# Keys before queries in the first batch, 1/rms spread through DRAM, and one add for the last shared expert tokens

## The chip, the cores and the metric

The kernel runs on one core of a Trainium2 chip. The metric is the device time of one execution in microseconds (us). A core has five engines that work through lists of their own: TensorE (PE; its weight loads are shown as PEld), VectorE (DVE), ScalarE (ACT), GpSimd (POOL) and SyncE (SP). DMAs are issued from the lists of SP, ACT and POOL ("SPq", "ACTq", "POOLq" in the profile) and move data beside them.

## The reference

Everything is float32. `x` is [4, 512, 512], the context [4, 1601, 512]; the first 257 context rows are image, the other 1344 text.

```python
def rms_norm(x, w):   # over all 512 features, before the heads are split
    return x * rsqrt(mean(x * x, -1) + 1e-6) * w

# 1. cross attention, 16 heads of 32
xl = layernorm(x)
q = rms_norm(xl @ q_w.T + q_b, norm_q_w)
k, v = rms_norm(ctx_txt @ k_w.T + k_b, norm_k_w), ctx_txt @ v_w.T + v_b
k_img, v_img = rms_norm(ctx_img @ k_img_w.T + k_img_b, norm_k_img_w), ctx_img @ v_img_w.T + v_img_b
x = x + (attention(q, k, v) + attention(q, k_img, v_img)) @ o_w.T + o_b    # two softmaxes

# 2. mixture of experts on layernorm(x): T = 2048 tokens, 32 experts
#    4 experts a token, chosen in the best 3 of 8 groups; at most 80 tokens an expert, in token order
out[token] += weight * down(silu(gate(x)) * up(x))       # routed experts, inner size 256
out += shared_down(silu(shared_gate(x)) * shared_up(x))  # shared expert, inner size 512
return x + out
```

## The kernel before, in words

The kernel writes its order out by hand: Python code appends instructions to the engines' lists, and nothing reorders them. PSUM is a ring of eight banks (`psum()`); a bank is used again when its readers are done. A float32 matmul of 512 columns stands in the trace as two records.

**Opening.** `first_x` loads four x tiles, then `wq` (four pieces), `first_wk`, `first_block` and the other weights, all from SP's queue; ScalarE's queue loads biases and norm weights (`column`, `bias_column`), 512 single floats each for a bias. `queries(0, ...)` gives for each x tile the steps `measure` (VectorE and GpSimd), `norm` (ScalarE, `xl`) and `turned` (transposes on TensorE, copied to `xlT` by ScalarE), and `work`, the four chunks of the query projection. All of it precedes the batch loop for batch 0; for later batches it is done in the batch before.

**Keys of one batch.** The keys are made transposed, features on partitions, in `BLOCKS` of 512, 512, 320 and 257 keys and four chunks of 128 features. `keys(bl, c)` makes one chunk: matmuls over four k (`feature_chunk`), then ScalarE squares the result (`sq`), VectorE adds the bias and multiplies by the norm weight (L228), GpSimd adds up the squares (L230). `norms` (in `side`: `N(x)`) sums the squares over partitions with a matmul against ones (L239), VectorE copies the sums out (L241) and GpSimd makes 1/rms of them (`inv_sqrt`, L196 and L197), as [128, 4]: one number for each key or query. `normed` (`M(x)`) has TensorE spread these numbers over all partitions (L250: a broadcast lhsT against the identity), and VectorE multiplies all four chunks with the result in PSUM (L253). `W(bl, qt)` are the scores of head group 0 for one block and one query tile: four matmuls in four banks (L299), whose largest values VectorE takes (L302). The table `side` says which of these steps follows which chunk; `select` are VectorE's routing steps of two batches before, seven behind a chunk. Then a list of steps follows: the rest of the scores, value tiles (`val`, copied from PSUM by ScalarE), for batches after the first the residual work of the batch before (`R(qt, i)`), `split` (VectorE) and `shifts`, which begins with transposes (L351).

**Attention.** For each of four chunks `c` of heads and 13 key tiles: exponentials on ScalarE (L366), weighted sums on TensorE (L373), denominators added up by GpSimd or VectorE (L381), the next chunk's scores (`wave`, L314 and L328).

**Experts.** `shared()` gives the steps of the shared expert for each 512 tokens: `gate`, `up`, `down`. The first three batches' steps are done before the routed experts. The 12 steps of the last (`between`: four gates, four ups, four downs) are spread through the loop over the routed experts. Such a `down` is copied from PSUM by ScalarE (`ys`) and added to `out` in DRAM by one of GpSimd's DMAs (L946). For a routed expert `gather(e)` fetches the rows of its tokens (L965, GpSimd's queue), `turn` transposes them (L976), `gate_up` and `down` are matmuls (L217, L995), ScalarE scales the result to `y` (L999), and an indirect DMA of GpSimd's queue adds it to `out` (L1000). Each DMA that adds to `out` waits until the one before has landed. `AHEAD` is how many experts ahead the rows are fetched, `WEIGHTS` how many experts' weights (1.5 MB each, from SP's queue) have a place.

Of the kernel before, what the change touches and what calls it, by code (L numbers as in the profile page):

```python
# [9 lines left out]
F32 = mybir.dt.float32  # L10
# [48 lines left out]
@with_exitstack  # L59
def xattn_moe_kernel(ctx: ExitStack, tc: tile.TileContext, a: dict, out: bass.AP):  # L60
    nc = tc.nc

    dram = ctx.enter_context(tc.tile_pool(name="dram", bufs=1, space=DRAM))
    x1_d = dram.tile([T, D], F32, name="x1_d")

    xw_d = dram.tile([T, D + E], F32, name="xw_d")
    xnT_d = dram.tile([P, NC, T], F32, name="xnT_d")
    den_d = dram.tile([B * NC, 2 * NG4, L], F32, name="den_d")
    rec_d = dram.tile([B * NC, 2 * NG4, L], F32, name="rec_d")

    const = ctx.enter_context(tc.tile_pool(name="const", bufs=1))
    ident = const.tile([P, P], F32, name="ident")
    make_identity(nc, ident)
    mhalf = const.tile([P, 8], F32, name="mhalf")
    nc.gpsimd.memset(mhalf, -0.5)
    logits = const.tile([P, NT, E], F32, name="logits")

    with tc.manual_schedule():
        body(tc, a, ident, mhalf, logits, x1_d, xw_d, xnT_d, den_d, rec_d, out)
# [30 lines left out]
def body(ctx, tc, a, ident, mhalf, logits, x1_d, xw_d, xnT_d, den_d, rec_d, out):  # L110
# [55 lines left out]
    def load_x(b, qt):  # L166
        xt = rowt("xt")
        nc.sync.dma_start(xt, a["x"][b, qt * P:(qt + 1) * P, :])
        return xt
# [64 lines left out]
    def norms(sq, n):  # L234

        nsub = -(-n // P)
        ps = psum()
        for s in range(nsub):
            nc.tensor.matmul(ps[:, s:s + 1], lhsT=sq[:, s * P:(s + 1) * P], rhs=ones[:, 0:1], start=True, stop=True)  # L239
        r = st.tile([P, 4], F32, name="rrms")  # L240
        nc.vector.tensor_copy(r[:, :nsub], ps[:, :nsub])  # L241
        inv_sqrt(r[:, :nsub], r[:, :nsub], 1.0 / D, 1e-6)
        return r

    def normed(dst, r, n):

        ps = psum()
        for s in range(-(-n // P)):
            m = min(P, n - s * P)
            nc.tensor.matmul(  # L250
                ps[:, s * P:s * P + m], lhsT=r[:, s:s + 1].to_broadcast([P, P]), rhs=ident[:, :m], start=True, stop=True
            )
        nc.vector.tensor_tensor(dst, dst, ps[:, :n].unsqueeze(1).to_broadcast([P, NC, n]), ALU.mult)  # L253
# [407 lines left out]
    routing_constants()  # L661
    select, search = [], []
    pending = []
    for b in range(B):
        kT = kv.tile([P, NC, S], F32, name="kT")
        v = kv.tile([P, NKT, P], F32, name="v", bufs=2)
        wk = first_wk if b == 0 else weight("k_w", wide("wk"))
        cTs = [first_block if b == 0 else load_block(b, 0), load_block(b, 1)]
# [12 lines left out]
        sqs, rs = {"q": sq_q}, {}  # L681

        if b > 1:
            space = kv.tile([P, NC, L], F32, name="space", tag="xlT")
            select, search = routing(b - 2, space.rearrange("p c t -> p (c t)"))
# [23 lines left out]
        def take_norms(x):  # L709
            rs[x] = norms(sqs[x], size(x))  # L710

        def take_normed(x):
            k0 = 0 if x == "q" else BLOCKS[x][0]
            normed(qT if x == "q" else kT[:, :, k0:k0 + size(x)], rs[x], size(x))
# [5 lines left out]
        def due():  # L720
# [5 lines left out]
        M = lambda x: partial(take_normed, x)  # L726
        W = lambda bl, qt: partial(scores, bl, qt)
        R = lambda qt, i: rest[qt][i] if b else lambda: None
        side = {
            (0, 0): [due, N("q")],  # L730
            (0, 1): [due],
            (0, 2): [M("q")],
            (1, 0): [N(0)],
            (1, 1): [val[0]],
            (1, 2): [M(0)],
            (1, 3): [W(0, 0)],
            (2, 0): [N(1), W(0, 1)],
            (2, 1): [W(0, 2), M(1)],
            (2, 2): [W(0, 3)],
            (2, 3): [W(1, 0)],  # L740
            (3, 0): [N(2), W(1, 1)],
            (3, 1): [W(1, 2), M(2)],
            (3, 2): [W(1, 3)],
            (3, 3): [W(2, 0)],
        }
# [11 lines left out]
        for f in [  # L757
            R(0, 0), val[1], W(2, 1), R(0, 1), N(3), W(2, 2), R(0, 2), R(1, 0), val[2], val[3], R(0, 3), M(3), W(2, 3),
            R(1, 1), val[4], R(1, 2), W(3, 0), R(2, 0), val[5], R(0, 4), R(1, 3), W(3, 1), R(2, 1), val[6], R(2, 2), val[7],
            W(3, 2), R(3, 0), R(1, 4), R(2, 3), val[8], W(3, 3), partial(split, mx, parts[0], NB), R(3, 1), val[9], val[10],  # L760
            R(2, 4), val[11], val[12],
        ]:
            f()
            if select:
                select.pop(0)()
# [120 lines left out]
    AHEAD, WEIGHTS = 6, 5  # L886
# [10 lines left out]
    def shared():  # L897
# [10 lines left out]
        for n in range(B):  # L908
# [22 lines left out]
            def down(j, n=n, t=t, fetch=fetch):  # L931
                rows = slice(n * L + j * P, n * L + (j + 1) * P)
                if n < BEFORE:
                    if j == 0:
                        fetch(0)
                    if j + 1 < NQ:
                        fetch(j + 1)
                ps = psum()
                project(ps, lambda k: t["hT"][:, k, j * P:(j + 1) * P], lambda k: sd[:, k, :])
                if n < BEFORE:  # L940
                    nc.vector.tensor_tensor(t[j], t[j], ps, ALU.add)
                    nc.sync.dma_start(out[rows, :], t[j])
                else:
                    y = held("ys")
                    nc.scalar.copy(y, ps)
                    nc.gpsimd.dma_start(out[rows, :], y, accum_op=ALU.add)  # L946
# [13 lines left out]
    def expert_parts():  # L960
# [31 lines left out]
        def down(e):  # L992
# [5 lines left out]
            y = ew.tile([CAP, D], F32, name="y")  # L998
# [15 lines left out]
    for u in units[:2]:  # L1014
# [11 lines left out]
    first, second = (  # L1026
        select + search
        for select, search in (routing(b, rp.tile([P, 1024], F32, name=f"space{b}")) for b in (B - 2, B - 1))
    )
# [7 lines left out]
    for i, u in enumerate(units):  # L1037
# [12 lines left out]
        later.step()  # L1050

# [9 lines left out]
    for e in range(E + 1):  # L1061
# [10 lines left out]
        while done < n_between and done * (E - 8) < n_between * (e + 1):  # L1072
# [39 lines left out]
```

## Time and profile before

| | |
|---|---|
| median of 3 runs (lowest to highest) | 1747.25 us (1747.18 to 1747.39) |
| the profiled execution: its time, its span | 1747.46 us, 1745.7 us |
| granted TensorE clock, mean | 0.993 |
| busy: PE, DVE, ACT, POOL | 1694.6, 982.5, 650.5, 866.9 us |
| moved by DMA | 137.34 MB |
| first gate_up of a routed expert, last matmul's start | 1495.74, 1719.64 us |

The profile is of one execution. "Busy" is the time in which an engine has an instruction under way; times in the trace count from the start of the span. A timeline line gives start, duration, engine, line of the kernel, operation, what it writes and reads, and how many were merged; in brackets stands the engine's idle time before it and what ended it. A line of windows gives for each engine its busy time and, in brackets, its instructions, then the granted clock, the share of the DMA engines' time and GB/s.

### The profile page before, as it was taken

What the parts mean: (1) busy time and instruction counts of PE and PEld (TensorE: products, weight loads), DVE (VectorE), ACT (ScalarE), POOL (GpSimd) and SP (SyncE); (2) the same over time, 40 slices, a digit from 0 to 9 for tenths busy, and PEclk for the clock granted to TensorE, in tenths of its full rate; (3) what the DMA queues carried; (4) which work ended last, traced back from release to release, by engine and by line L of the source; (5) the groups of instructions that cost most, each with busy time, mean ns of one, the idle gap of its engine ahead of it and who ended that gap; (6) DMA issues with size and microseconds to landing.
All of it is one profiled execution on the core that took longest, in us unless ns stands there. A gap on an engine that the chain in (4) does not pass through costs nothing. (4 is left out here: it accounts for less than half of the span.)

```text
span 1745.7 us, 29525 instructions
## 1 busy us (share of the span) xinstructions
PE 1694.6 (97%) x11825; PEld 893.7 (51%) x11825; DVE 982.5 (56%) x2016; ACT 650.5 (37%) x1378; POOL 866.9 (50%) x618
## 2 busy tenths in 40 slices
PE   6999999999999999999999999999999999999984
PEld 3564444446544444565444445644443454677763
DVE  2675555758555548976666579676557666111100
ACT  2124556621354566114555641145557110011111
POOL 2328879332569763336688533286792110333232
PEclk9999999999999999999999999999999999999997
DMA  6000000221100004020000040300012462688882
GB/s 228 1 2 1 26 20 8 93 82 55 43 2 26 26 3 150 26 79 19 5 23 26 15 149 20 103 13 14 2 39 86 159 229 86 204 264 265 262 253 38
DMA packets 67912, 137.34 MB, mean 79 GB/s; under 512 B 16064, under 2 KB 28480, under 8 KB 65600
## 3 DMA queue, kind: packets, MB, share of 16 engines
q1 hardware_dynamic: 58720, 123.30, 20.8%
q0 software_dynamic: 5696, 11.87, 3.3%
q8 instruction: 93, 1.52, 0.4%
q10 hardware_dynamic: 3360, 0.30, 0.1%
q14 instruction: 43, 0.35, 0.1%
HBM read 112.63 MB, written 22.81 MB: 78 GB/s over the span
## 5 line engine op out<-in xcount | busy, mean ns | idle before, releaser
L366 ACT ACTIVATE pT<-ps 128x512 f32<-128x512 f32 (+1 forms) x832 | 429.7, 603 | 342.2 <-PE ps L365 334.1
L328 DVE TENSOR_REDUCE mx<-ps 128x1 f32<-128x512 f32 (+1 forms) x576 | 331.3, 617 | 264.8 <-PE ps L314 264.8
L381 POOL TENSOR_TENSOR acc<-acc,pT 128x1024 f32<-128x1024 f32 x192 | 445.7, 2359 | 3.0 <-ACT pT L366 2.6
L373 PE MATMUL po<-pT,v 128*32 128x512 f32 (+2 forms) x1792 | 222.0, 603 | 0.0
L284 PEld LDWEIGHTS ps<-v_w,cT 128*128 128x128 f32 (+1 forms) x1408 | 168.9, 186 | 102.2 <-DVE mx L328 56.1
L365 PE MATMUL ps<-qT,kT 32*128 32x512 f32 (+1 forms) x1664 | 213.7, 587 | 0.0
L314 PE MATMUL ps<-kT,qT 32*128 32x512 f32 (+1 forms) x1536 | 206.2, 549 | 0.0
L284 PE MATMUL ps<-v_w,cT 128*128 128x128 f32 (+1 forms) x1408 | 197.7, 284 | 0.0
L223 PE MATMUL ps<-cT,wk 128*128 128x512 f32 (+1 forms) x384 | 153.7, 545 | 0.0
L302 DVE TENSOR_REDUCE mx<-ps 128x1 f32<-128x512 f32 (+2 forms) x256 | 128.3, 564 | 5.7 <-PE ps L299 5.6
L1000 POOL DMA_INDIRECT out<-y,tok x32 | 45.7, 1428 | 143.9 <-ACT y L999 55.6
L990 DVE TENSOR_TENSOR ehT<-ehT,ps 128x160 f32<-128x160 f32 x32 | 10.3, 322 | 181.9 <-ACT ehT L989 148.2
L362 PEld LDWEIGHTS <-pick 32*128 32x128 bf16 (+1 forms) x832 | 21.6, 91 | 165.8 <-issue 164.0
L223 PEld LDWEIGHTS ps<-cT,wk 128*128 128x128 f32 x384 | 69.6, 190 | 69.0 <-issue 54.3
L292 ACT COPY v<-ps 128x128 f32<-128x128 f32 (+1 forms) x208 | 59.7, 287 | 118.3 <-PE ps L284 117.8
L230 POOL TENSOR_TENSOR sq_k<-sq_k,sq 128x512 f32<-128x512 f32 (+2 forms) x48 | 49.7, 1035 | 105.3 <-ACT sq L227 105.1
L388 POOL TENSOR_TENSOR acc<-pT 128x1024 f32<-128x1024 f32 x24 | 56.2, 2361 | 87.1 <-ACT pT L366 54.5
L381 POOL TENSOR_TENSOR pT<-pT 65x1024 f32<-65x1024 f32 x24 | 56.0, 2355 | 86.5 <-PE po L373 77.8
L381 DVE TENSOR_TENSOR acc<-acc,pT 128x1024 f32<-128x1024 f32 (+1 forms) x72 | 97.8, 1405 | 2.1 <-ACT pT L366 2.1
L314 PEld LDWEIGHTS ps<-kT,qT 32*128 32x128 f32 x1536 | 82.0, 183 | 30.8 <-issue 10.1
L373 PEld LDWEIGHTS po<-pT,v 128*32 128x32 f32 (+2 forms) x1792 | 34.7, 107 | 118.6 <-issue 109.3
L362 PE MATMUL ps<-mT,pick 32*128 32x512 bf16 (+1 forms) x832 | 82.5, 385 | 2.5 <-ACT mT L353 2.5
(176 smaller groups left out, 2220.0 us busy)
## 6 DMA issues: line engine op xcount, KB each, us to landing
W_gate<-in_W_gate SPq DMA_DIRECT2D x32, 512.0 KB
W_up<-in_W_up SPq DMA_DIRECT2D x32, 512.0 KB
W_down<-in_W_down SPq DMA_DIRECT2D x32, 512.0 KB
xt<-in_x SPq DMA_DIRECT2D x32, 256.0 KB
cT<-in_ctxT SPq DMA_DIRECT2D x8, 1024.0 KB
rb<-rec_d SPq DMA_DIRECT2D x64, 128.0 KB
wk<-in_k_w SPq DMA_DIRECT2D x4, 1024.0 KB
wki<-in_k_img_w SPq DMA_DIRECT2D x4, 1024.0 KB
```

What stands on the lines that cost most here:

```text
L223: nc.tensor.matmul(ps[:, :n], lhsT=wt[:, k, c * P:(c + 1) * P], rhs=xT[:, k, to], start=k == 0, stop=k == NC - 1)
L284: nc.tensor.matmul(ps[lo:hi, :], lhsT=cTs[bl][:, k, at:at + hi - lo], rhs=ws[bl == NB - 1][:, k, c * P:(c + 1) * P], start=k == 0, stop=k ...
L292: nc.scalar.copy(v[:n, t, :], ps[:n])
L302: nc.vector.tensor_reduce(mx[:, qt, g, bl:bl + 1], ps[:, :n], AX.X, ALU.max, negate=True)
L314: nc.tensor.matmul(ps[:, j * n:(j + 1) * n], lhsT=qT[r:r + HD, c, q * P:(q + 1) * P], rhs=kT[r:r + HD, c, k0:k0 + n], start=True, stop=True,)
L328: nc.vector.tensor_reduce(mx[:, qt, g, i:i + 1], ps[:, :m], AX.X, ALU.max, negate=True)
L362: nc.tensor.matmul(ps[:n], lhsT=pick[r:r + HD, kind(t), :n], rhs=mT[r:r + HD, :], start=True, stop=False)
L365: nc.tensor.matmul(ps[:n], lhsT=kT[r:r + HD, c, t * P:t * P + n], rhs=qT[r:r + HD, c, :], start=False, stop=True)
L366: nc.scalar.activation(pT[:n, g, :], ps[:n], AF.Exp)
L373: nc.tensor.matmul(po[r:r + HD, :], lhsT=v[rows, t, r:r + HD], rhs=pT[rows, g, :], start=start, stop=stop)
L381: (nc.vector if idle else nc.gpsimd).tensor_tensor(to[rows, h, :], to[rows, h, :], pT[rows, h, :], ALU.add)
L388: (nc.vector if idle else nc.gpsimd).tensor_tensor(acc[:, h, :], pTs[0][:, h, :], pTs[1][:, h, :], ALU.add)
```

## The change

Four things change, in the text below in this order.

- The first batch begins with keys. `k_w` and the first context block are loaded in four pieces each, by ScalarE's and SP's queues side by side, with the x tiles between them and the biases behind them. The first block's key chunks are made k by k in four banks ahead of the loop, with the norms and turns of x between them; the query chunks (`work[c]`) take the place of that block's `keys` in the loop.
- `norms` becomes four parts: the sums and 1/rms as before (`N`), a DMA of ScalarE's queue that writes the 512 numbers to DRAM one by one (`N1`), a DMA of the same queue that reads them back on all 128 partitions (`N2`), and the multiply, which reads them from SBUF, first for one chunk (`M`), then for the other three (`M1`). TensorE's part in it (L250) is gone. The first scores stand behind chunk (2, 0), not (1, 3).
- The four `down`s of the last shared tokens are copied into one tile and added to `out` by one DMA, and the 12 steps are spread over fewer experts (`E - 15` for `E - 8`). `AHEAD` is 7 for 6, `y` has four buffers for three.
- The routing constants are made in batch 1, and the two last routings take their space one at a time, the second in the tile `rb`.

```diff
+    rms_d = dram.tile([B * (NB + 1), 512], F32, name="rms_d")
...
-    first_x = [load_x(0, qt) for qt in range(NQ)]
+    first_wk = wide("wk")
+    _, n, s0, _ = BLOCKS[0]
+    first_block = cx.tile([P, NC, n], F32, name="cT0", tag="cT0")
     wq = w.tile([P, NC, D], F32, name="q_w")
+    first_x = []
+    for k in range(NC):
+        nc.scalar.dma_start(first_wk[:, k, :], a["k_w"][:, k, :])
+        nc.sync.dma_start(first_block[:, k, :], a["ctxT"][0, k * P:(k + 1) * P, s0:s0 + n])
+        if k in (1, 2):
+            first_x += [load_x(0, len(first_x), nc.scalar), load_x(0, len(first_x) + 1)]
     for k in range(NC):
         nc.sync.dma_start(wq[:, k, :], a["q_w"][:, k, :])
+    k_b, nk_w = bias_column("k_b"), column("norm_k_w")
     q_b, nq_w = bias_column("q_b"), column("norm_q_w")
-    k_b, nk_w = bias_column("k_b"), column("norm_k_w")
-    first_wk = weight("k_w", wide("wk"))
-    first_block = load_block(0, 0)
+    second_block = load_block(0, 1)
...
     def norms(sq, n):
         nsub = -(-n // P)
-        ps = psum()
-        for s in range(nsub):
-            nc.tensor.matmul(ps[:, s:s + 1], lhsT=sq[:, s * P:(s + 1) * P], rhs=ones[:, 0:1], start=True, stop=True)
+        to = rms_d[norms_taken.pop(0), :nsub * P]
         r = st.tile([P, 4], F32, name="rrms")
-        nc.vector.tensor_copy(r[:, :nsub], ps[:, :nsub])
-        inv_sqrt(r[:, :nsub], r[:, :nsub], 1.0 / D, 1e-6)
-        return r
-
-    def normed(dst, r, n):
-        ps = psum()
-        for s in range(-(-n // P)):
-            m = min(P, n - s * P)
-            nc.tensor.matmul(
-                ps[:, s * P:s * P + m], lhsT=r[:, s:s + 1].to_broadcast([P, P]), rhs=ident[:, :m], start=True, stop=True
-            )
-        nc.vector.tensor_tensor(dst, dst, ps[:, :n].unsqueeze(1).to_broadcast([P, NC, n]), ALU.mult)
+        got = []
+        def sums():
+            ps = psum()
+            for s in range(nsub):
+                nc.tensor.matmul(ps[:, s:s + 1], lhsT=sq[:, s * P:(s + 1) * P], rhs=ones[:, 0:1], start=True, stop=True)
+            nc.vector.tensor_copy(r[:, :nsub], ps[:, :nsub])
+            inv_sqrt(r[:, :nsub], r[:, :nsub], 1.0 / D, 1e-6)
+        def out_():
+            nc.scalar.dma_start(to.rearrange("(s p) -> p s", p=P), r[:, :nsub])
+        def back():
+            got.append(cx.tile([P, 512], F32, name="rrms_b"))
+            nc.scalar.dma_start(got[0][:, :nsub * P], to.partition_broadcast(P))
+        return sums, out_, back, got
+    def normed(dst, r, n, chunks):
+        nc.vector.tensor_tensor(
+            dst[:, chunks, :], dst[:, chunks, :], r[:, :n].unsqueeze(1).to_broadcast([P, chunks.stop - chunks.start, n]), ALU.mult
+        )
...
-    for _, norm, turned in turn:
-        norm()
-        turned()
-    nc.vector.tensor_scalar(nq_w, nq_w, SM_SCALE, None, ALU.mult)
-    for f in work:
-        f()
+    first_kT = kv.tile([P, NC, S], F32, name="kT")
+    first_banks = [psum() for _ in range(NC)]
+    for k in range(NC):
+        if k == NC - 1:
+            first_sq = rowt("sq_k")
+            nc.vector.tensor_scalar(nq_w, nq_w, SM_SCALE, None, ALU.mult)
+        for c, ps in enumerate(first_banks):
+            feature_chunk(first_kT[:, :, :n], first_block, n, first_wk, k_b, nk_w, c, ps, first_sq if k == NC - 1 else None, k)
+        if k == 0:
+            turn[0][1]()
+            turn[1][1]()
+        if k == 2:
+            for qt in (0, 1):
+                turn[qt][2]()
+                turn[qt + 2][1]()
+    for qt in (2, 3):
+        turn[qt][2]()
...
+        x0, x1 = ("q", 0) if b else (0, "q")
         side = {
-            (0, 0): [due, N("q")],      (0, 1): [due],           (0, 2): [M("q")],
-            (1, 0): [N(0)],             (1, 1): [val[0]],        (1, 2): [M(0)],          (1, 3): [W(0, 0)],
-            (2, 0): [N(1), W(0, 1)],    (2, 1): [W(0, 2), M(1)], (2, 2): [W(0, 3)],       (2, 3): [W(1, 0)],
-            (3, 0): [N(2), W(1, 1)],    (3, 1): [W(1, 2), M(2)], (3, 2): [W(1, 3)],       (3, 3): [W(2, 0)],
+            (0, 0): [due, N(x0)],             (0, 1): [due, N1(x0)],      (0, 2): [N2(x0)],          (0, 3): [M(x0), M1(x0)],
+            (1, 0): [N(x1)],                  (1, 1): [N1(x1), val[0]],   (1, 2): [N2(x1)],          (1, 3): [M(x1)],
+            (2, 0): [W(0, 0), N(1), M1(x1)],  (2, 1): [W(0, 1), N1(1)],   (2, 2): [W(0, 2), N2(1)],  (2, 3): [W(0, 3), M(1)],
+            (3, 0): [W(1, 0), N(2), M1(1)],   (3, 1): [W(1, 1), N1(2)],   (3, 2): [W(1, 2), N2(2)],  (3, 3): [W(1, 3), M(2)],
         }
         for bl in range(NB):
             for c in range(NC):
-                keys(bl, c)
+                if b == 0 and bl == 0:
+                    work[c]()
+                else:
+                    keys(bl, c)
...
         for f in [
-            R(0, 0), val[1], W(2, 1), R(0, 1), N(3), W(2, 2), R(0, 2), R(1, 0), val[2], val[3], R(0, 3), M(3), W(2, 3),
-            R(1, 1), val[4], R(1, 2), W(3, 0), R(2, 0), val[5], R(0, 4), R(1, 3), W(3, 1), R(2, 1), val[6], R(2, 2), val[7],
+            R(0, 0), val[1], W(2, 0), M1(2), R(0, 1), N(3), W(2, 1), R(0, 2), N1(3), val[2], R(1, 0), W(2, 2), val[3],
+            N2(3), R(0, 3), W(2, 3), R(1, 1), M(3), val[4], R(1, 2), W(3, 0), M1(3), R(2, 0), val[5], R(0, 4), R(1, 3),
+            W(3, 1), R(2, 1), val[6], R(2, 2), val[7],
...
-    AHEAD, WEIGHTS = 6, 5
+    AHEAD, WEIGHTS = 7, 5
...
-                    y = held("ys")
-                    nc.scalar.copy(y, ps)
-                    nc.gpsimd.dma_start(out[rows, :], y, accum_op=ALU.add)
+                if j == 0:
+                    t["ys"] = wide("ys")
+                nc.scalar.copy(t["ys"][:, j, :], ps)
+                if j == NQ - 1:
+                    to = out[n * L:(n + 1) * L, :].rearrange("(j p) d -> p j d", p=P)
+                    nc.gpsimd.dma_start(to, t["ys"], accum_op=ALU.add)
...
-            y = ew.tile([CAP, D], F32, name="y")
+            y = ew.tile([CAP, D], F32, name="y", bufs=4)
...
-        while done < n_between and done * (E - 8) < n_between * (e + 1):
+        while done < n_between and done * (E - 15) < n_between * (e + 1):
```

(The entries of `side` are set several to a line here.)

More of the change, by code (lines that the diff above doesn't have):

```diff
@@ L78, in xattn_moe_kernel @@
     with tc.manual_schedule():
-        body(tc, a, ident, mhalf, logits, x1_d, xw_d, xnT_d, den_d, rec_d, out)
+        body(tc, a, ident, mhalf, logits, x1_d, xw_d, xnT_d, rms_d, den_d, rec_d, out)
 BEFORE = 3
@@ L109, in body @@
 @with_exitstack
-def body(ctx, tc, a, ident, mhalf, logits, x1_d, xw_d, xnT_d, den_d, rec_d, out):
+def body(ctx, tc, a, ident, mhalf, logits, x1_d, xw_d, xnT_d, rms_d, den_d, rec_d, out):
     nc = tc.nc
@@ L164, in weight, with load_x @@
         return t
[L166 removed]
+    def load_x(b, qt, queue=nc.sync):
         xt = rowt("xt")
[L168 removed]
+        queue.dma_start(xt, a["x"][b, qt * P:(qt + 1) * P, :])
         return xt
@@ L681, in body @@
         sqs, rs = {"q": sq_q}, {}
+        if b == 0:
+            sqs[0] = first_sq
+        if b == 1:
+            routing_constants()
         if b > 1:
@@ L1025, in body @@
     rest = [residual(B - 1, qt, aoT_last, lambda: wo) for qt in range(NQ)]
[L1026 to L1029, printed above, removed]
+    first, second = sum(routing(B - 2, rp.tile([P, 1024], F32, name="space")), []), None
     O_AT = 8
@@ L1050, in body @@
         later.step()
+        if i == ready:
+            space = mid.tile([P, 2, L], F32, name="rb")
+            second = sum(routing(B - 1, space.rearrange("p k t -> p (k t)")), [])
         while spent < (i - 1) * SHARE and (first or i > ready and second):
```

55 lines of the change are left out of this document (31 added, 24 removed).

## The prediction

> **What bounds the kernel now.** I read the page first, then TensorE's timeline through one batch's keys, the windows of that stretch, the opening, and last GpSimd's queue at the end.
>
> ```profile
> PE 1694.6 (97%) x11825; PEld 893.7 (51%) x11825; DVE 982.5 (56%) x2016; ACT 650.5 (37%) x1378; POOL 866.9 (50%) x618
> ```
>
> TensorE is busy for 97%, so a microsecond taken from its list counts, unless another engine then turns up late. About 51 us of its span are idle: 14 in the opening, 6 at 1689, 22 behind its last matmul.
>
> The opening (timeline):
>
> ```profile
> 4.07 0.33 ACTq L155 DMA_DIRECT2D norm_k_img_w<-in_norm_k_img_w  x1
> 7.38 1.28 ACT L265 ACT_TABLE_LOAD   x1 [7.38 <-DMA norm_k_img_w<-in_norm_k_img_w]
> ...
> 18.84 16.82 PE L223 MATMUL ps<-xlT,q_w 128*128 128x512 f32 x32 [0.68 <-ACT xlT L272]
> ```
>
> The first real matmul starts at 18.84; before it TensorE only turned four x tiles (4 x 1.12 us).
>
> Keys of batch 0, TensorE:
>
> ```profile
> 63.11 1.05 PE L250 MATMUL ps<-ident,rrms 128*128 128x128 f32 x8
> 64.00 3.60 PE L223 MATMUL ps<-cT,wk 128*128 128x512 f32 x8
> ```
>
> and the windows of that stretch (PE, PEld, DVE, ACT, POOL):
>
> ```profile
> 69.00:116.00 47.00, 47.00 (x327) 32.63 (x326) 41.92 (x86) 6.95 (x19) 9.13 (x15) 1.00 0.01 1
> ```
>
> The spreading of 1/rms (L250) costs TensorE 0.89 us from its start to the next matmul. But from the first scores on (L299), VectorE is busy 41.9 of 47 us: TensorE leads, with little to spare.
>
> The end, GpSimd:
>
> ```profile
> 1688.01 0.96 POOL L946 DMA_DIRECT2D out<-ys  x1 [3.34 <-DMA out<-y,tok]
> 1689.28 0.99 POOL L965 DMA_INDIRECT xp<-xw_d,tok  x1 [0.30 <-issue]
> 1695.44 1.47 POOL L1000 DMA_INDIRECT out<-y,tok  x1 [5.18 <-DMA out<-ys]
> ...
> 1733.22 1.40 POOL L1000 DMA_INDIRECT out<-y,tok  x1 [3.26 <-DMA out<-y,tok]
> 1737.92 1.40 POOL L1000 DMA_INDIRECT out<-y,tok  x1 [3.30 <-issue]
> ```
>
> Each add to out waits until the one before has landed. This chain, not TensorE (last matmul 1723.2), ends the kernel.
>
> **The opening.** TensorE could start when 512 KB are in. The four x tiles (256 KB) land 1.03 us apart, the first at 4.07 (VectorE's L202 starts), so two land at about 5.1. The 32 key records then take what the 32 query records take now, 18.84 to 35.08 = 16.2 us with the slow start: done at 21.3. Four turns at full speed are 4 x 0.65: 24.0. The loop, now entered at 35.51, would begin 11.5 earlier. Bytes don't forbid it: 3 MB of keys, context and x at 1.03 per 256 KB are in at about 15.
>
> What speaks against it is ScalarE's queue. Its six large loads and nine small ones stand ahead of its first activation, and at most eight hardware DMAs are in flight: the ninth now waits (norm_k_img_w is issued at 4.07, when the first x lands; the fourth x tile waits 2.2 us for q_b, 3.5 us from issue to landing). With eight in flight the small ones wait for tiles landing at 9.3, 11.3, 13.4 and 15.4, and the last four for other small ones: ScalarE is free at about 21, has its table at 22.3 and the first xl at 23.1. TensorE, done with three quarters of the keys at 5.1 + 3 x 3.43 + 3 (slow start) = 18.4, waits 4.7. Behind the turns ScalarE also squares the keys before it copies xlT: about 1 more. Gain 11.5 - 4.7 - 0.8 = 6. Bounds: 11.5 with no such wait; 2 if the slow clock comes back in the pause: after the 5.9 us idle at 1689 four L995 records took 3.62 us instead of 1.88. The Trainium skill ("TensorE: Matmul & The Clock Gate", Part 1: The HAM clock gate) says that one idle window of about 3.4 us is enough for half rate; by it the gain would be nearer 3, and the trace, with no pause between 1.8 and 5.9 us in it, does not decide.
>
> **1/rms through DRAM.** L250 goes: 0.89, 0.89, 0.99, 0.71 and 0.66 us from start to next matmul in batch 0, 4.1 per batch, 16.6 in all, on TensorE's path. Added are 40 DMA issues on ScalarE, 0.46 each by q_b's row (also 512 single floats) = 18 us on an engine at 37%: hidden. But the issues wait: the write for GpSimd's L197, the read for the write's landing. Behind them on ScalarE stand the next Square and v copies, and on those VectorE's L228, GpSimd's L230 and TensorE's banks. Write to landing: between den_d's 2.2 us (698.20 to dn's issue at 700.42) and q_b's 3.5; I take 3.3, for single floats. Reading 256 KB back: 3.0, between rb's 2.8 and the first x tile's 3.3. A key chunk is 3.4, so one part per step mostly fits.
>
> VectorE's multiply (L253, 2.28 us) now reads the row from SBUF, not PSUM, in two pieces; L381's 128x1024 at best 1.22 against half of 2.28 makes it 7% longer. A dearer price: L573, two SBUF inputs, has a median of 292 ns and a maximum of 1353, beside a GpSimd tensor_tensor at 706.4.
>
> ```profile
> L573 DVE TENSOR_TENSOR space<-space x16: 284/292/1353, 706.7 to 1442.7; 128x128 f32<-128x128 f32 x16
> ```
>
> The Trainium skill ("SBUF — State Buffer", Who interferes with whom) has the rule: an instruction with two SBUF inputs contends with a GpSimd instruction that reads SBUF; one with a single SBUF input, as L253 is now, does not. By it each of the 20 multiplies could lose up to one L230 (0.73 to 1.27 us). From L573's row (median against maximum) I count 0.3 each, about 1.5 per batch, inside the waits below.
>
> VectorE now paces. In blocks 2 and 3 it has, after the change, eight score groups of 2.42, eight L228 (4 x 0.53, 4 x 0.46), 1.7 + 0.6 + 1.1 + 0.4 of multiplies: about 28 us. TensorE without L250 has 9.1 + 7.6 keys, 8 x 1.07 scores, 1.5 norms: 26.7. So it waits about 1.5, and another 2 where W(1,0) and W(2,0) follow a multiply queued behind a group of reductions. Batches 1 to 3: 4.1 - 3.5 = 0.6 gained each; bounds 4.1 gained (no wait) and 2.5 lost (3 us more of collisions and late rows). Batch 0 has no residual work in its tail: from N(3), sums to multiply take 0.2 + 1.2 + 3.3 + 0.5 + 3.0 = 8.2 us at least, against three groups of 1.64 on VectorE, so 3.3 more of waiting, part of it under the 1.6 that split has spare: 1.8 lost; bounds 3 gained, 6 lost. Sum: 3 x 0.6 - 1.8 = 0. Where the freed 16.6 go: into waits for VectorE.
>
> **Scores one part later, routing_constants, SBUF moves.** W(0,0) comes one chunk (2.3) later, counted above in VectorE's sum. The constants' 0.6 us of GpSimd and one DMA lie beside other work: zero, at most 0.6. The second routing space in rb: zero, rb is read long before.
>
> **The end.** Four adds of 256 KB took 8.3, 7.5, 7.8 and 7.4 us of GpSimd's chain from their start to the next scatter (31). One of 1 MB: between 7.4 (size free) and 31; a scatter of 160 KB lands in 3.9, 256 KB in 5.7 median, so I take 14: 17 saved. But twelve pieces now end with expert 15, not 22. Scatter 14 left 115.6 us after the first gate_up (1495.74); three more pieces of 3.44 lie before it: 125.9. Its landing (6), the 1 MB (14): scatter 15 at 146. While weights load, chained scatters stand 4.8 to 8.3 apart, mean 6.6 (16 to 21); nine of them: 206; seven at 4.68: 238; and 7.8 from the last scatter to the span's end: 246 to 248 against 250 now. Gain 2 to 4, say 2. Bounds: TensorE alone (32 x 5.53 + 12 x 3.44 = 218, then 13 to the end) 19 gained; 7.5 apart and 24 for the add: 14 lost. AHEAD 7 and four y buffers let TensorE run further ahead (5.9 at 1689 go), but that is not what ends last.
>
> **Sum.** The span of the profiled execution is 1745.7, its time 1747.46; the median of the runs shown is 1747.25, 0.2 below. 6 + 0 + 2 = 8 less: 1739.
>
> **Rivals.**
> 1. TensorE keeps what it is given: 11.5 in the opening, 13 of L250, 5 at the end: 1718. For it: 97% busy. Against: 41.9 of 47. Chance 0.22.
> 2. The round trip takes the place of L250. If write and read together last over 8 us instead of 6.3 (loads of 2.2 MB are in flight where N("q") falls), or the multiplies collide with GpSimd, each batch loses 3 and batch 0 seven: 16 lost, 8 gained elsewhere: 1755, slower. It decides from a pair of 8 us on. For it: VectorE waits in order, and its reductions empty the banks. Against: one chunk's slack per part. Chance 0.17.
> 3. The end turns: bare experts (5.53 of TensorE) outrun scatters 7 us apart: 11 lost there, 6 gained in the opening: 1752. Chance 0.13.
> That the change doesn't do what it says can't be: L250 is gone from the program.
>
> **How the numbers follow.** The forecast has 0.48. About 0.2% (3.5 us) is what a measurement of this kernel can tell from no change. The forecast with its spread of 5 is faster in 0.82 of cases, same in 0.14; rival 1 always faster, rival 2 always slower, rival 3 half slower, 0.35 same: faster 0.63, same 0.11, slower 0.26. The range reaches into rivals 1 and 2: 1719 to 1756; the forecast's own is 1732 to 1746.
>
> **What would show it.** Right: the loop's first query chunk near 29.5; no L250; TensorE in batch 0 waiting for kT or qT (VectorE) at the scores, most at W(3,0); one add from ys, about 14 us to the next scatter; scatters 6 to 7 apart while weights load. Wrong: turns waiting for nothing and the loop at 24; scores never waiting; TensorE pausing for GpSimd's gathers; a batch longer than now by more than 3.

## The result and the profile after

The changed kernel takes 1873.76 us (median of 4 runs, 1869.69 to 1883.86) where the kernel before, run beside it, takes 1747.32 us (1747.18 to 1747.47): a ratio of 1.0735, 95% interval 1.0699 to 1.0772. The prediction said 1739, with 1719 to 1756 as its range. The profiled execution took 1869.69 us, its span is 1868.0 us, its granted clock 0.955 (before: 0.993).

The page of the changed kernel, engines and the clock in 40 slices:

```profile
PE 1727.0 (92%) x11681; PEld 900.4 (48%) x11681; DVE 988.7 (53%) x2036; ACT 647.5 (35%) x1378; POOL 873.5 (47%) x615
...
PEclk9879999997899999988999999799999999999997
```

The 144 records of L250 are gone (11825 records before), and yet TensorE's busy time is 32 us longer: the instructions that are left ran at a lower clock. The dips of the clock stand where the keys of the four batches are made.

The opening is better than predicted. TensorE's timeline (start, duration, engine, line, operation; in brackets the idle time before):

```profile
5.73 13.44 PE L232 MATMUL ps<-cT,wk 128*128 128x512 f32 x24 [5.73 <-DMA wk<-in_k_w]
19.00 1.35 PE L290 MATMUL ps<-ident,xl 128*128 128x128 f32 x8
...
26.38 3.70 PE L232 MATMUL ps<-xlT,q_w 128*128 128x512 f32 x8 [1.71 <-ACT xlT L291]
```

Keys run without a pause from 5.73 on, the first turns (L290) follow at 19.00, and the loop begins at 26.38 instead of 35.51: 9.1 us earlier. The one pause behind 5.73, 1.71 us for ScalarE's copies of `xlT`, left the granted clock at 1.00 (26.38 to 34).

The loss lies in the keys. From the loop's start to the first transposes of `shifts` batch 0 takes 142.69 - 26.38 = 116.3 us (before 116.18 - 35.51 = 80.7). From the sums of N("q") to the same transposes, batches 1 to 3 take 130.0, 131.9 and 134.0 us (before 98.6, 99.6, 100.6). That is 35.6 + 31.5 + 32.3 + 33.4 = 132.8 us. The attention between (237.5 us in batch 0 in both) did not change.

One part of batch 0 on ScalarE's queue, the write of 1/rms (L258), the read (L262), the first step behind them, and VectorE's multiply that uses the row:

```profile
115.68 0.37 ACTq L258 DMA_DIRECT2D rms_d<-rrms  x1
123.91 0.34 ACTq L262 DMA_DIRECT2D rrms_b<-rms_d  x1
124.29 0.27 ACT L311 COPY v<-ps 128x128 f32<-128x128 f32 x1 [5.30 <-DMA rms_d<-rrms]
```

```profile
128.56 0.43 DVE L270 TENSOR_TENSOR kT<-kT,rrms_b 128x257 f32<-128x257 f32 x1 [7.41 <-DMA rrms_b<-rms_d]
```

From the write's issue to the read's, which waits for the write to land, it is 8.2 us (8 to 10 in all parts), and the row is used 4.7 us after the read's issue: 12.9 us for the pair. TensorE then stands before the scores (timeline, batch 0), and the waits add up (engine, what waits, for whom: us in all, times, longest):

```profile
89.66 1.75 PE L318 MATMUL ps<-kT,qT 32*128 32x512 f32 x8 [3.88 <-DVE kT L270]
110.14 1.45 PE L318 MATMUL ps<-kT,qT 32*128 32x320 f32 x8 [5.31 <-DVE kT L270]
129.04 1.24 PE L318 MATMUL ps<-kT,qT 32*128 32x257 f32 x8 [8.51 <-DVE kT L270]
```

```profile
PE ps L318 <- DVE kT L270: 81.8, 15, 8.6
ACT sq L236 <- DMA rms_d<-rrms: 56.3, 10, 9.0
DVE kT L270 <- DMA rrms_b<-rms_d: 30.9, 13, 7.4
```

The multiply that ends the pause of 3.88 us started at 88.92, with VectorE's reductions directly ahead of it:

```profile
88.92 0.68 DVE L270 TENSOR_TENSOR kT<-kT,rrms_b 128x512 f32<-128x512 f32 x1
```

A pause like this is paid twice. The windows of TensorE around it (last three columns: granted clock, DMA share, GB/s):

```profile
84.00:88.00 4.00, 1.78 (x8) 1.20 (x7) 2.00 (x4) 0.89 (x2) 1.00 (x2) 1.00 0.38 53
88.00:92.00 4.00, 2.35 (x11) 0.97 (x12) 2.65 (x5) 0.00 (x0) 0.00 (x0) 0.76 0.04 13
92.00:96.00 4.00, 4.00 (x12) 3.13 (x12) 3.62 (x6) 0.00 (x0) 1.87 (x2) 0.50 0.00 0
96.00:100.00 4.00, 4.00 (x21) 2.27 (x24) 2.79 (x5) 0.72 (x2) 1.35 (x2) 0.89 0.05 0
```

Behind the pause the clock is low until about 96: the eight key records (L232, 257 columns) that start at 92.64 take 3.71 us up to the next instruction, the eight that start at 97.65 take 1.94.

The multiplies also meet GpSimd. The first step of its 1/rms (L205), 0.19 us in the kernel before and in 12 of the 20 parts, takes 1.63 us in the other eight, and each time a multiply of three chunks is under way on VectorE:

```profile
71.66 1.75 DVE L270 TENSOR_TENSOR qT<-qT,rrms_b 128x1536 f32<-128x1536 f32 x1
71.83 1.63 POOL L205 TENSOR_SCALAR rrms<-rrms 128x4 f32<-128x4 f32 x1 [7.68 <-DVE rrms L254]
```

What these 1.4 us per part cost the whole kernel, no run shows.

### The profile page after: what moved, and what is told of

It reads as the page before. It is cut to its first block, busy times and chain, and to the rows that moved or that the text cites. A ratio compares the mean times of both kernels' runs of the same rounds, so it can differ in the third digit from the quotient of the medians.

```text
span 1868.0 us, 29308 instructions
## 1 busy us (share of the span) xinstructions
PE 1727.0 (92%) x11681; PEld 900.4 (48%) x11681; DVE 988.7 (53%) x2036; ACT 647.5 (35%) x1378; POOL 873.5 (47%) x615
## 5 line engine op out<-in xcount | busy, mean ns | idle before, releaser
L303 PEld LDWEIGHTS ps<-v_w,cT 128*128 128x128 f32 (+1 forms) x1408 | 173.8, 190 | 107.7 <-DVE mx L347 56.1
L303 PE MATMUL ps<-v_w,cT 128*128 128x128 f32 (+1 forms) x1408 | 203.8, 290 | 0.0
L232 PE MATMUL ps<-cT,wk 128*128 128x512 f32 (+1 forms) x384 | 163.1, 577 | 5.7 <-DMA wk<-in_k_w 5.7
L318 PE MATMUL ps<-kT,qT 32*128 32x512 f32 (+2 forms) x512 | 77.5, 672 | 85.7 <-DVE kT L270 81.8
L232 PEld LDWEIGHTS ps<-cT,wk 128*128 128x128 f32 x384 | 75.7, 204 | 83.1 <-issue 65.0
L239 POOL TENSOR_TENSOR sq_k<-sq_k,sq 128x512 f32<-128x512 f32 (+2 forms) x48 | 49.5, 1031 | 123.1 <-ACT sq L236 106.6
```

The source lines that it names most:

```text
L232: nc.tensor.matmul(ps[:, :n], lhsT=wt[:, k, c * P:(c + 1) * P], rhs=xT[:, k, to], start=k == 0, stop=k == NC - 1)
L303: nc.tensor.matmul(ps[lo:hi, :], lhsT=cTs[bl][:, k, at:at + hi - lo], rhs=ws[bl == NB - 1][:, k, c * P:(c + 1) * P], start=k == 0, stop=k ...
L318: nc.tensor.matmul(ps[:, :n], lhsT=qT[r:r + HD, c, qt * P:(qt + 1) * P], rhs=kT[r:r + HD, c, k0:k0 + n], start=True, stop=True)
```

## The experiments

Theories as they stood after the result: the write of single floats makes the round trip too long (A); against it ScalarE's blocked queue, the changed order of the steps, the opening, or the end. Each chip's runs of the kernel before had a median between 1747.6 and 1748.5 us. Differences between runs are of medians.

**e1: no row through DRAM.** `N`, `M`, `side` and the list are those of before; opening and end stay changed.

```diff
...
-        return sums, out_, back, got
...
+        return r
...
```

L250's spreading by TensorE is back, and the multiply reads from PSUM.

> The changed kernel, with 1/rms spread by TensorE as before (L250's matmuls, and the order of steps in side and in the list behind it as before); opening and end as changed. Theory A (the round trip through DRAM alone costs 33 us in each batch, opening and end gain 9 and 1): about 1737, below the kernel before. Rival (the loss comes from the parts meeting, such as the later scores with the new opening or the larger AHEAD): well above 1747.

Measured 1740.05 us (1738.78 to 1742.07), ratio 0.9950 [0.9933, 0.9966]. The whole loss is in the rows and in the order that came with them: 1873.76 - 1740.05 = 133.7 us.

**e2: the rows alone, on the kernel before.** `norms`, `normed`, `side` and the list of the change, nothing else of it.

```diff
...
-            (0, 0): [due, N("q")], (0, 1): [due], (0, 2): [M("q")], ...
+            (0, 0): [due, N("q")], (0, 1): [due, N1("q")], (0, 2): [N2("q")], (0, 3): [M("q"), M1("q")], ...
```

> The kernel before with only the four-part 1/rms through DRAM and its order of steps. Theory A: 1747 + 4 x 33 = 1880. Rival (part of the loss is the opening's): clearly less, the more so in batch 0.

Measured 1907.93 us (1898.80 to 1910.04), ratio 1.0898 [1.0865, 1.0931]: 160 us lost, not 133, and more than theory A's 1880. The write is slower here too, for example 87.32 to 96.32 in batch 0 and 1246.32 to 1259.31 in batch 3. Why the same write takes some 1 us longer in this kernel stays open.

**e3: pieces of 16 B.** Partition p writes its four numbers side by side; the multiplies read the row with a stride.

```diff
-            nc.scalar.dma_start(to.rearrange("(s p) -> p s", p=P), r[:, :nsub])
+            nc.scalar.dma_start(to.rearrange("(p s) -> p s", p=P), r[:, :nsub])
```

> The changed kernel, but the write lays the four numbers of a partition side by side: 128 pieces of 16 bytes instead of 512 of 4 (the multiply reads them with a stride, and takes a part block in two instructions). Theory A1 (the write's 8 to 10 us are the number of its pieces): from the write's issue to the read's about 3 us, pair about 7, no more than 5 us lost per batch: 1737 to 1757. Rival A2 (a write to DRAM that is read back lasts this long whatever its pieces): still about 8 us, and 1874.

Measured 1776.52 us (1772.98 to 1783.85), ratio 1.0162 [1.0127, 1.0196]: between theory A1 (up to 1757) and A2 (1874). 97 us come back with fewer pieces, although the multiplies get dearer. ScalarE's queue in this run:

```profile
67.06 0.33 ACTq L258 DMA_DIRECT2D rms_d<-rrms  x1
68.64 0.33 ACTq L262 DMA_DIRECT2D rrms_b<-rms_d  x1
```

1.6 us from write to read here, the shortest (up to 4.2, where the read also stands behind other steps). The multiply of three chunks costs 2.92 us with the stride (1.74 in the changed kernel), so the 36 us above e1 could be its price or something else.

**e4: the opening alone, on the kernel before.**

```diff
...
-                keys(bl, c)
+                if b == 0 and bl == 0:
+                    work[c]()
+                else:
+                    keys(bl, c)
```

> The kernel before with the new opening alone (keys first, loads in pieces on two queues). Theory A: the loop's first query chunk starts at 26.4 instead of 35.5 and nothing is given back: 1738. Rival (later loads or routing come too late in batch 0 and take it back): 1742 to 1747.

Measured 1739.76 us (1739.00 to 1741.88), ratio 0.9955 [0.9938, 0.9971]. The opening brings 8 us; with e1 at 1740.05 the changed end brings nothing.

**e5: the order without DMAs.** The changed kernel's order, but the two DMAs (N1, N2) do nothing, TensorE spreads 1/rms at M's place, and VectorE multiplies all four chunks there, in one instruction from PSUM.

```diff
...
-            rs[x][i]()
+            pass
...
```

> The changed kernel with its order of steps kept (scores one part later, 1/rms asked for one chunk later, the list behind the loop), but nothing goes through DRAM: where M stood, TensorE spreads the 1/rms and VectorE multiplies from PSUM, as in the kernel before. Theory A, the round trip alone is what costs: within 4 us of the run without rows, 1736 to 1744. Theory B, the order itself costs part of it (the 36 us that 16-byte pieces left over): 1755 to 1775.

Measured 1784.46 us (1780.07 to 1791.11), ratio 1.0211 [1.0180, 1.0242]. Theory A alone falls, and the time lies above theory B's range too: this order loses 44 us against e1 with no DMA at all. VectorE and TensorE in this run, batch 0:

```profile
75.77 2.47 DVE L311 TENSOR_REDUCE mx<-ps 128x1 f32<-128x512 f32 x4
78.16 2.28 DVE L262 TENSOR_TENSOR kT<-kT,ps 128x2048 f32<-128x2048 f32 x1
```

```profile
76.58 1.90 PE L232 MATMUL ps<-cT,wki 128*128 128x257 f32 x8
80.49 1.53 PE L308 MATMUL ps<-kT,qT 32*128 32x512 f32 x8 [2.01 <-DVE kT L262]
98.53 0.82 PE L308 MATMUL ps<-kT,qT 32*128 32x320 f32 x8 [2.19 <-DVE kT L262]
```

In `(2, 3): [W(0, 3), M(1)]` the multiply stands behind W(0, 3)'s reductions, and the scores that need it come one chunk of 1.90 us later. But e5 is not the change without its DMAs. The first scores need one chunk only; the changed kernel multiplies that one first, in 0.69 us (0.49 for 320 keys, 0.43 for 257), while e5's scores wait for all four, 2.28 us (1.48 and 1.21). An estimate from these rows: with the short multiplies in place of the long ones, e5's 16 pauses of this kind would add up to 9.5 us instead of 27.8. No run tried the divided multiply with a row in time, so how much of the 44 us belongs to the change is not shown.

Behind the pause of 2.01 us the clock drops (windows of the same run):

```profile
78.00:80.40 2.40, 0.48 (x3) 0.08 (x1) 2.40 (x3) 0.48 (x1) 0.00 (x0) 1.00 0.00 0
80.40:84.00 3.60, 3.51 (x16) 2.26 (x17) 2.47 (x6) 0.00 (x0) 0.00 (x0) 0.60 0.00 0
84.00:88.00 4.00, 4.00 (x16) 2.36 (x14) 0.93 (x3) 0.48 (x1) 1.38 (x3) 0.51 0.00 0
```

Behind the longer one before 98.53, 2.19 us, it stays at 1.00 up to 106.

The four keys stages (N("q")'s sums to `shifts`), added up from the windows:

| | stages | TensorE busy | idle |
|---|---|---|---|
| e1, order of before | 362.0 | 356.6 | 5.4 |
| e5, new order, no DMA | 404.6 | 376.7 | 27.9 |
| the changed kernel | 491.7 | 393.6 | 98.0 |

e5 has e1's TensorE work, so by difference 22.5 us of its loss are pauses and 20.1 the clock behind them. The changed kernel has 16.6 less of work (L250): 92.7 of pauses, and 37.0 + 16.6 = 53.6 of clock.

**e6: rows of 512 B.** TensorE turns the numbers, the write is four pieces, the row lies in order.

```diff
...
+            nc.tensor.transpose(ps[:nsub, :P], r[:, :nsub], ident)
...
+            nc.vector.tensor_copy(got[0][:nsub, :P], ps[:nsub, :P])
-            nc.scalar.dma_start(to.rearrange("(s p) -> p s", p=P), r[:, :nsub])
+            nc.scalar.dma_start(to.rearrange("(s p) -> s p", p=P), got[0][:nsub, :P])
```

> The changed kernel; before the write TensorE turns the 128x4 numbers into 4 rows of 128 and VectorE copies them out, so that the write is 4 pieces of 512 B, and the row comes back in order (the multiplies read it without a stride). Theory A, the write's time goes by its pieces: write to issue of the read 2 to 3 us, multiplies 0.69 and 1.75 us again; 20 turns and copies of some 0.5 us beside it: 1742 to 1758. Theory C, any pair of DMAs is too long for this order (what 16-byte pieces left over is the read): 1765 to 1785.

Measured 1782.45 us (1776.75 to 1783.58), ratio 1.0189 [1.0166, 1.0212].

```profile
69.56 0.27 ACTq L262 DMA_DIRECT2D rms_d<-rrms_b  x1
70.80 0.33 ACTq L265 DMA_DIRECT2D rrms_b<-rms_d  x1
```

1.2 us for four pieces here (1.1 to 4.6 in all parts). The time lies in theory C's range, but it does not show that the pair of DMAs is what holds this kernel up: TensorE waits 23.7 us at the added turn, which itself waits for GpSimd's 1/rms, and 22.2 at the scores for the multiply. e3 and e6 end near e5, 8 and 2 us below it, but each of the three carries a price of its own.

**e7: both DMAs from SP's queue.**

```diff
-            nc.scalar.dma_start(to.rearrange("(s p) -> p s", p=P), r[:, :nsub])
+            nc.sync.dma_start(to.rearrange("(s p) -> p s", p=P), r[:, :nsub])
-            nc.scalar.dma_start(got[0][:, :nsub * P], to.partition_broadcast(P))
+            nc.sync.dma_start(got[0][:, :nsub * P], to.partition_broadcast(P))
```

> The changed kernel with both DMAs of each row issued from SP's queue instead of ScalarE's, all else the same. Theory A, the late row itself is what TensorE waits for (scores behind the multiply): the time stays near that of the change, 1850 to 1885. Theory D, ScalarE standing still behind its write (its squares and copies come 3.6 to 9 us late, 56 us in sum by the profile) is what costs: 1780 to 1820.

Measured 1906.99 us (1903.69 to 1910.84), ratio 1.0902 [1.0884, 1.0921]: worse by 33. ScalarE no longer stands behind the write, and nothing is won: its blocked queue by itself is not what costs. The write takes about 9 us from this queue (76.02 to 85.18) and the row is used 4.8 us after the read's issue (89.95): a pair of 13.9 us in place of 13.0 in the same part of the changed kernel (75.93 to 88.92, there behind the reductions). Whether this longer pair is all of the 33 us stays open.

**e8: sums on all partitions at once**, on e4: one matmul against 128x128 ones, 1/rms by ScalarE.

```diff
...
+        nc.tensor.matmul(ps[:, :n], lhsT=ones, rhs=sq[:, :n], start=True, stop=True)
+        nc.scalar.activation(r[:, :n], ps[:, :n], AF.Ln, bias=epsD)
+        nc.scalar.activation(r[:, :n], r[:, :n], AF.Exp, scale=-0.5)
```

> The kernel before with the new opening; the sums over partitions are made on all partitions at once by one matmul against a 128x128 matrix of ones (about 0.86 us for 512 columns, by the key records), in place of the 128x1 sums (0.95) and the spreading (0.89): about 1 us of TensorE freed per part, 20 in all, with no DMA. ScalarE makes 1/rms of them (Ln, then Exp of -0.5 times it), which brings 38 more table loads of 1.28 us on ScalarE; no GpSimd step. Theory of rival 1, TensorE keeps what it is given: 1720 to 1728. Theory of the forecast, in the keys stage another engine then ends last: 1736 to 1750; above 1750 if ScalarE's table loads hold the squares up.

Measured 1741.89 us (1738.99 to 1746.38), ratio 0.9968 [0.9958, 0.9978], e4 had 1739.76. TensorE's freed time was not kept. That VectorE paces is not shown by it, since ScalarE's table loads hold the squares up: GpSimd waits 153.9 us for them (e4: 105.8). The multiplies, which read the row from SBUF here too, also meet GpSimd: at 69.28 its sum of 320 squares (L240) took 2.47 us beside one, at 72.70 it took 0.86 alone.

**e9: e5 with the multiply ahead of the score group.**

```diff
-            (2, 3): [W(0, 3), M(1)],
+            (2, 3): [M(1), W(0, 3)],
-            (3, 3): [W(1, 3), M(2)],
+            (3, 3): [M(2), W(1, 3)],
-            N2(3), R(0, 3), W(2, 3), R(1, 1), M(3), val[4], ...
+            N2(3), R(0, 3), M(3), W(2, 3), R(1, 1), val[4], ...
```

> The run with the order alone (1784), with the multiply put ahead of the score group that stood before it in three places (blocks 1, 2 and 3), all else the same. Theory E, the order costs because the multiply stands behind 2.5 us of reductions on VectorE directly ahead of the scores that need it (pauses of some 2 us at the first scores of each block, and a lower clock behind them): 1738 to 1750. Theory F, it is the later scores themselves, which fall into the list behind the loop: 1770 to 1785 still.

Measured 1748.17 us (1746.77 to 1751.19), ratio 1.0003 [0.9993, 1.0013]. VectorE at the same place:

```profile
75.40 2.28 DVE L262 TENSOR_TENSOR kT<-kT,ps 128x2048 f32<-128x2048 f32 x1
77.60 2.48 DVE L311 TENSOR_REDUCE mx<-ps 128x1 f32<-128x512 f32 x4
```

Theory E holds for e5: 36 of its 44 us were the place of its multiply, the undivided one.

**e10: e6 with the same three moves (the diff of e9).**

> The run with rows of 512 B (1782), with the first multiply put ahead of the score group before it in the same three places. Theory E: with a short write and the multiply in time the rows through DRAM cost little: 1735 to 1750, and if TensorE keeps the L250 records that it is freed of (16.6 us, less 20 turns of 0.28) 1730. Theory C, the pair of DMAs is late at this place, so that the reductions behind the multiply now wait too: 1780 or more.

Measured 1775.28 us (1771.54 to 1776.49), ratio 1.0161 [1.0145, 1.0178]. It does not decide: the turn that e6 added is what TensorE waits at (waits of this run; 23.7 us in e6):

```profile
PE ps L259 <- POOL rrms L206: 30.4, 15, 3.3
```

**e11: the 12 shared steps over `E - 8` experts**, on e1.

```diff
-        while done < n_between and done * (E - 15) < n_between * (e + 1):
+        while done < n_between and done * (E - 8) < n_between * (e + 1):
```

> The run without rows (1740), with the 12 shared steps spread over as many experts as before the change (E - 8 for E - 15), so that one add of 1 MB takes the place of four adds of 256 KB at the place of the last of them. Theory of the forecast's step, GpSimd's chain of adds ends the kernel and one add of 16 us in place of 31 us shortens it: 1725 to 1736. Theory of rival 3, scatters do not follow TensorE any faster: 1738 to 1745.

Measured 1731.34 us (1731.28 to 1731.79), ratio 0.9909 [0.9892, 0.9925]: the fastest version of all, 8.7 us below e1. One add is worth something, but at its old place.

**e12: pieces of 16 B in key order, multiply early.** Partition p sums keys 4p to 4p+3, so no step is added and no multiply has a stride; the weight loads of the sums now have one. Beside this diff those of e3's write and of e9.

```diff
-                nc.tensor.matmul(ps[:, s:s + 1], lhsT=sq[:, s * P:(s + 1) * P], ...)
+                nc.tensor.matmul(ps[:, s:s + 1], lhsT=sq[:, :nsub * P].rearrange("q (p s) -> q s p", s=nsub)[:, s, :], ...)
```

> The changed kernel with three edits: partition p sums keys 4p to 4p+3 (weight loads of the sums with a stride), so that a write of 128 pieces of 16 B lies in key order and the multiplies read the row without a stride; and the multiply ahead of the score group in the three places. No step of TensorE waits for 1/rms. Theory G, the loss of the change is the time of the single-float write and the multiply's place, and the path through DRAM as such costs nothing: 1730 to 1750. Theory C, the pair of DMAs holds the row up at any size of piece: 1770 or more.

Measured 1775.61 us (1773.54 to 1776.58), ratio 1.0155 [1.0138, 1.0172]. It is 27 us above e9, without single floats and without a turn: in theory C's range and outside G's. TensorE in batch 0:

```profile
92.56 1.40 PE L318 MATMUL ps<-kT,qT 32*128 32x320 f32 x8 [2.07 <-DVE kT L270]
106.05 1.62 PE L318 MATMUL ps<-kT,qT 32*128 32x257 f32 x8 [3.59 <-DVE kT L270]
```

The rows of blocks 2 and 3 still come late: VectorE waits 28.4 us in all for rows, and TensorE 18.3 at the scores for the multiply. But part of the 27 us is this run's own. The strided weight loads make the sums dearer, here those of the queries in e9 and in e12:

```profile
45.17 0.95 PE L248 MATMUL ps<-ones,sq_q 128*128 128x1 f32 x8
45.23 1.80 PE L253 MATMUL ps<-ones,sq_q 128*128 128x1 f32 x8
```

All sums take TensorE 32.3 us in place of 18.4. In the four keys stages, 27.9 us longer than e9's, pauses make 18.0 and TensorE's busy time 9.9. Also, at 59.87 a multiply of one chunk that starts under GpSimd's sum of squares (L239, 59.25 to 60.52) takes 1.20 us, where it took 0.69 in the changed kernel. So theory C stands by the waits, but 14 us less would lie between the two ranges, and what the pair of DMAs costs by itself is not shown. That the list behind the loop has too little work between to cover write and read is an argument, and no run tried it.

**e13: the changed kernel with the three moves (the diff of e9), single floats kept.**

> The changed kernel, with single floats, and only the multiply ahead of the score group in the three places. Theory G: the row lands some 13 us after its write is issued, behind that place too, so that now the reductions wait with the multiply: 1860 to 1900. Theory E alone (the multiply's place is what costs, whatever the write takes): 1830 to 1845, the 36 us that the same edit brought to the order alone.

Measured 1905.98 us (1903.83 to 1909.50), ratio 1.0903 [1.0883, 1.0923]: the move that brought 36 us in e5 costs 32 here, a little above the range of theory G. VectorE now waits for the row with the reductions queued behind it (waits):

```profile
DVE kT L270 <- DMA rrms_b<-rms_d: 84.7, 16, 14.1
```

**e14: e12 with the shared steps over `E - 8` (the diff of e11).**

> The run of 16-byte pieces in key order with the multiply early, and the 12 shared steps over E - 8 experts. By the run with the early add against the one without rows, 9 us less than its partner without that edit; by theory G it is 1722 to 1741 and may pass 1731.

Measured 1770.44 us (1767.75 to 1772.85), ratio 1.0132 [1.0115, 1.0149]: 5 us below e12, not 9, and far from e11.

The account of the change, in medians: the opening 8 us gained (e4), the end nothing (e1 against e4), the rows and their order 133.7 lost (e1). Of these, at least 97 belong to the write of single floats (e3, whose dearer multiplies stand against its gain). The other 36 are not taken apart: e5, e6 and e12, which each leave out a part of the change, each bring a cost of their own.

## Why the prediction was wrong, by its own steps

- **The write to landing, taken as 3.3 us**, between den_d's 2.2 and the 3.5 of q_b's load: this step failed. It measured 8 to 10, and e3 shows what that is worth: at least 97 us. q_b's 512 single floats are read from DRAM, and a read was taken as the nearest row for a write; den_d's write has larger pieces. No row of the trace before was a write of single floats, so 3.5 was no upper end. The read back, taken as 3.0, was 3.6 to 5.0 where the multiply waited for it, and the pair 12.9 for 6.3.
- **VectorE's waits, 3.5 us per batch.** TensorE waited 85.7 us at the scores for the multiply (81.8 for keys, 3.9 for queries), 21 per batch: with the row that late, this term went too. The slow clock behind the pauses, 53.6 us or 13 per batch, had no term in this part, though the prediction had one for it in the opening. Whether the order alone would have cost more than 3.5 stays open. The text named the place ("where W(1,0) and W(2,0) follow a multiply queued behind a group of reductions") and gave it 2 us; e5 and e9 show that this place can cost 9 us per batch, but with an undivided multiply, and the estimate at e5 leaves pauses of 2.4 per batch for a divided one. The sum itself has a slip: its terms for VectorE add up to 27.1 us, not about 28, so that by them the first wait was 0.4 and not 1.5.
- **L250 gone, 16.6 us freed.** True of TensorE's list, but no run shows it kept: e3, freed of it, ends 8 us below e5, which is not, and e8 kept nothing of a like amount.
- **ScalarE's blocked issues.** They were taken as a danger, and e7 shows that they alone are not the cause: with ScalarE free the row is as late, and the time is longer still.
- **The multiply, 7% longer from SBUF.** Right: 0.69 + 1.74 = 2.43 us for L253's 2.28. The collision with GpSimd, which the Trainium skill ("SBUF — State Buffer", Who interferes with whom) makes possible, came, and the trace agrees with the page; but in the changed kernel it is GpSimd that loses, not VectorE. The mean of the 128x1536 multiplies is 1744 to 1750 ns, and L205 takes 1.63 us for 0.19 in eight of 20 parts. The prediction's 0.3 us each was put on the multiplies; the 1.4 us stand ahead of the write, where the prediction had no term for them.
- **The opening, 6 us.** Too small: 9.1 at the loop, 8 in e4. ScalarE's table load began at 16.63, not about 21, so the turns waited for nothing. The bound of 2, a slow clock behind a pause, did not come up: the one pause, 1.71 us, left the clock at 1.00. The 16.2 us for 32 records run to the start of the last one; to its end (35.51) they are 16.7.
- **The end, 2 us.** Measured 1.2 from the first gather on (257.7 before, 256.5 after) and nothing in e1 against e4. The add took 16.3 us to the next scatter (1752.19 to 1768.50) for 14. That three more pieces ahead of the add eat its gain was right, and e11 shows the other side: without them 8.7 us come back.
- **The rivals.** Rival 2 was the case, with its mechanism and its point of decision (a pair over 8 us), but with 16 us lost (3 per batch, 7 in batch 0) where 132.8 were measured (31 to 36 in each): its pair lasts 12.9 us and not just over 8, and the slow clock was no part of it. Its other condition, multiplies that collide with GpSimd, came as well, at GpSimd's cost. Rival 1's 1718 was reached by no run; e11 comes nearest. Rival 3's bare experts did not outrun the scatters into a loss.
- **What would show it.** "Most at W(3,0)" was right (8.51 us), and so was the sign against the forecast, a batch longer by more than 3. Another sign against it, turns waiting for nothing, came for a good reason: ScalarE was free earlier, and the loop began at 26.38, between the 24 of that sign and the 29.5 of the forecast.

## What to carry to other kernels

Price a DMA by the size of its pieces and by its direction, from a row that has both; where the trace has none, keep the upper end open, and ask for how many steps of the list the result may be late. Where two in-order engines feed each other, an instruction that the other engine needs soon goes ahead of long work that nobody waits for (e9), but only if its own input is there (e13). Count a pause of TensorE with the slow clock that can stand behind it: 20.1 us on 22.5 of pauses in e5, 53.6 on 92.7 in the changed kernel. And when a run takes one part of a change out, check the length of what it puts in its place: e5's multiply and e12's sums were longer than what they stood for.

## What the runs showed of the hardware

512 floats written to DRAM took 8 to 10 us as single floats in the changed kernel, 1.6 us at the shortest in 128 pieces of 16 B (e3), and 1.1 us at the shortest in four of 512 B (e6), while q_b's load of 512 single floats landed in 3.5. The Trainium skill ("DMA: Bandwidth & Descriptors", Specifications) says that pieces under 512 B are read, changed and written back. The runs agree that small pieces are slow; that this is the reason, no run shows.

A pause of 2.01 us was followed by a granted clock of 0.60 and 0.51 over the next 7.6 us (e5), one of 2.19 us in the same batch by 1.00. The Trainium skill ("TensorE: Matmul & The Clock Gate", Part 1: The HAM clock gate) puts the fall behind one idle window of about 3.4 us. Here a shorter pause was enough in one place and not in another, so a pause below that figure can cost time, its length alone does not tell whether it will, and the measurement decides.

A VectorE multiply that reads both inputs from SBUF and a GpSimd instruction beside it did not share: the one that started second ended with, or after, the first. L205 took 1.63 us under a multiply of 1.75 and 0.19 alone (the changed kernel); a multiply of one chunk took 1.20 us under GpSimd's sum of squares in e12 and 0.69 in the changed kernel, with no such sum beside it.
